# Layer 2 of image 0: the symmetric half for 10 of its 28 block pairs, in five transposed runs among the taps of layer 1, with column sums added by transfers

## The chip, the cores and the metric

The kernel runs on one core of a Trainium2 chip. The metric is the device time of one execution in microseconds (us), the median of several. The core has five engines with an instruction queue each: TensorE (PE, matrix products; its weight loads are shown as PEld), VectorE (DVE), ScalarE (ACT), GpSimd (POOL) and SyncE (SP, which here only issues transfers). Each engine works through its own queue in order and meets the others at semaphores. Data lie in SBUF (128 partitions); products go to PSUM.

## The reference, cut to what matters

Four images of 64 x 64 positions and 64 channels pass through four layers: an attention (layer 0), a convolution block (layer 1: norm, two pointwise products with a depthwise 3x3 convolution between them, a gate, and a second norm with two more pointwise products), a second attention without any weights (layer 2), and a last one (layer 3). The change is in layer 2:

```python
def _L2_conv_ref(x):
    B, C, H, W = x.shape
    N = H * W
    xf = x.reshape(B, C, N)
    scores = jnp.einsum('bci,bcj->bij', xf, xf)
    attn = jax.nn.softmax(scores, axis=-1)
    out = jnp.einsum('bcj,bij->bci', xf, attn).reshape(B, C, H, W)
    return out + x
```

The sum over c runs over the 64 rows, i and j over the 4096 pairs of the other two axes. The matrix of scores is the product of a matrix with itself, so it is symmetric, and so is its exponential before the division by the row sums: the block (g, h) is the transpose of the block (h, g).

## The kernel before, in words

The program is written out by hand as one list of items. A stage (layer 0, 2 or 3 of an image) appends items; `at(i, fn)` hangs work behind item i. Beside them run two lanes of generators, `conv` (layer 1 of an image) and `misc` (small things such as `features2`, which makes the copy `ko` that layer 2 takes its scores from). A lane has a clock: `tick(us)` moves it on by what an item is said to last, each `yield us` in the generator says how much clock its piece takes, and a piece is issued when the clock has come to it. So the numbers in `tick` and `yield` set the places at which layer 1's instructions stand between those of the stage, on every engine.

The order of stages is: layer 0 of the images 0 to 3; layer 2 of image 0; then layer 2 of image 1, layer 3 of image 0, layer 2 of image 2, and so on. Layer 1 of image b is run by the lane `conv` beside the stage after its layer 0. Layer 1 of image 3 therefore falls into layer 2 of image 0. In it `norm` (L1164 to L1191) sends eight broadcasts through SP, `pointwise` with pw1 is written to a padded tile by ACT (L1222), and the depthwise convolution is done by DVE: for each of two halves r and four column groups j nine taps, k = 0 to 8, over 128 x 1024 elements (the first at L1236, the others at L1238 and L1241), each adding to the one before. Then come the gate (L1249), a second `norm`, and pw3 and pw4 (L1205, L1284 to L1293).

Layer 2 divides the 4096 columns into eight blocks of 512. A block takes two steps. One step is a group of four 64x512 score products on PE into one 128x1024 PSUM slot, its exponential on ACT into a tile `e`, and a group of four 64x512 products of x with `e`. A group shows as eight records in the trace, PE's products being in two passes.

- Image 0 uses `layer2` (L1312 to L1372): all 8 x 8 blocks in 128 steps (32 items of four), 32 steps for each 1024 columns. The exponential is one ACT instruction of 128x1024 (L1336). The products (L1348) of 32 steps stay in a pair of PSUM accumulators; at their end ACT copies one, DVE adds the other (L1356), PE turns the result with four transposes (`turn`, L1361) and DVE copies it (L1364). `close2` (L1375 to L1385) divides by the row sums; it runs in four places of the next stage and has no PE work.
- The images 1 to 3 use `layer2s`: 72 steps. Of each pair of blocks only one is made; the products with the transposed block are made from `turned`, a copy of `e` with its 32x32 squares transposed by DVE (L1458, one instruction a step), by `turned_products` (L1509: 64 products, a "transposed run", for four steps). The two groups of accumulators are added by DVE into a tile A in SBUF (L1483). POOL adds the tiles `e` of a row block into `esum` (L1469, L1471), since the row sums of the transposed blocks are the column sums of these; `spread_sums` brings them to `cs` on DVE (L1477, L1478). `weights` (L1423) lays x out for the runs by 16 transfers of 32 KB on SP for each row block. A is cleared by POOL (L1539). `close2s` (L1556 to L1580) has four small products, 32 PE transposes, four multiplications and eight additions.

Tiles come from pools that are used in turn: `new_e` gives one of six buffers of 128x2048 (two steps to a buffer), `new_acc` the one pair of accumulators, `new_big` one of five large tiles, `new_ps` a PSUM slot. A buffer is written again only when everything that reads it is done.

Of the kernel before, what the change touches and what calls it, by code (L numbers as in the profile page):

```python
# [691 lines left out]
def fast_path(ctx: ExitStack, tc: tile.TileContext, a: dict, out: bass.AP, bad):  # L692
# [392 lines left out]
    def layer0(b):  # L1085
# [51 lines left out]
        def item(t):  # L1137
            tiles[t] = (
                [new_e() for _ in range(2)], sm.tile([128, C], F32, tag="vq", name="vq", bufs=4),
                sm.tile([128, 4], F32, tag="zs", name="zs", bufs=4),  # L1140
            )
            for g in range(4):
                if g == 2 and between:
                    between.pop()()
                score(t, g)
                late.append(lambda g=g: product(t, g))
                conv.tick(2.3)
                misc.tick(1.8)
                if g == 0 and t:
                    scale(t - 1)  # L1150
                follow()
            if t == 31:
                scale(t)
# [45 lines left out]
    def layer1(b):  # L1199
# [16 lines left out]
        for r in (1, 0):  # L1216
# [11 lines left out]
            for j in range(4):  # L1228
                w0 = 16 * j
                y1 = new_t("y1").rearrange("p (w h) -> p w h", h=H)  # L1230
                for k in range(9):
# [3 lines left out]
                    if k == 0:  # L1235
# [9 lines left out]
                    yield 1.8  # L1245
# [66 lines left out]
    def layer2(b):  # L1312
        x, m, first = X[:, b], im[b], len(items)
        xw = x.rearrange("p (w h) -> p w h", h=H)
        m.ph = None
        m.zs = sm.tile([128, 32, 4], F32, tag="zs2", name="zs2")
        es, acc = {}, {}
        quads = ((0, 0), (1, 0), (0, 1), (1, 1))

        def scores(n):  # L1320
            ib = n // 8
            if n == 0 and b:
                take_slots(0, 1, 2)
            for jb in range(4 * (n % 8), 4 * (n % 8) + 4):
                ps = new_ps()
                for r, c in quads:
                    rows_ = slice(64 * r, 64 * r + 64)
                    mm(  # L1328
                        ps[64 * c : 64 * c + 64, bass.ts(r, 512)],
                        m.ko[rows_, 128 * jb + 64 * c : 128 * jb + 64 * c + 64],  # L1330
                        m.ko[rows_, bass.ts(2 * ib + r, 512)], start=True, stop=True,
                    )
                if jb % 2 == 0:
                    e = new_e()
                es[n, jb] = e[:, bass.ts(jb % 2, 1024)]
                act(es[n, jb], ps, AF.Exp, bias=SHIFT2, accum_out=m.zs[:, jb, ib : ib + 1])  # L1336
                follow(0)
                conv.tick(2.5)
                misc.tick(1.8)

        def products(n):
            ib = n // 8
            if n % 8 == 0:
                acc[0], acc[1] = new_acc(), new_acc()
            for jb in range(4 * (n % 8), 4 * (n % 8) + 4):
                for r, c in quads:
                    rows_ = slice(64 * r, 64 * r + 64)
                    mm(  # L1348
                        acc[r][64 * c : 64 * c + 64, :], xw[rows_, jb, :],
                        es[n, jb][rows_, bass.ts(c, 512)], start=jb == 0, stop=jb == 31,  # L1350
                    )
            if n % 8 == 7:
                if m.ph is None:
                    m.ph = new_big("ph")
                nc.scalar.copy(m.ph[:, 2048:2560], acc[0])
                nc.vector.tensor_add(m.ph[:, 2048:2560], m.ph[:, 2048:2560], acc[1])  # L1356

        def turn(ib):
            ps = new_ps()
            for i in range(4):  # L1360
                nc.tensor.transpose(  # L1361
                    ps[:, bass.ts(i, 128)], m.ph[:, 2048 + 128 * i : 2176 + 128 * i], ident
                )
            nc.vector.tensor_copy(  # L1364
                m.ph[:, bass.ts(ib, 512)].rearrange("p (r q h) -> p q r h", r=2, q=4),
                ps[:, 0:512].rearrange("p (q r h) -> p q r h", q=4, r=2),
            )

        for n in range(32):
            items.append((lambda n=n: scores(n), 0.0))  # L1370
            at(first + n + (2 if n == 0 and b > 1 else 1), lambda n=n: products(n))
            if n % 8 == 7:  # L1372
                at(first + n + 2, lambda n=n: turn(n // 8))

    def close2(b):  # L1375
        x, m = X[:, b], im[b]
        nc.vector.tensor_reduce(sums2[:, b, :], m.zs, AX.X, ALU.add)
        rz = sm.tile([128, 32], F32, tag="rz2", name="rz2")
        nc.vector.reciprocal(rz, sums2[:, b, :])
        for i in range(4):  # L1380
            d = m.ph[:, bass.ts(i, 512)].rearrange("p (w h) -> p w h", h=H)
            nc.vector.tensor_mul(d, d, rz[:, bass.ts(i, 8)].unsqueeze(2).to_broadcast([128, 8, H]))
            xs = x[:, bass.ts(i, 512)]
            nc.vector.tensor_add(xs, xs, m.ph[:, bass.ts(i, 512)])
            yield 2.0 if i < 3 else 9.0  # L1385

    SIDES = [[(7, (h + 1) % 7), ((h + 2) % 7, (h + 3) % 7)] for h in range(7)] + [[]]  # L1390

    def layer2s(b, when_free):
# [5 lines left out]
        used = {}  # L1398
        steps = []
        for h in (7, 0, 1, 2, 3, 4, 5, 6):  # L1400
            own = [(h, h, u, None, None) for u in range(2)]
            other = [
                (h, g, u, pi, 2 * gi + u)
                for pi, pair in enumerate(SIDES[h]) for gi, g in enumerate(pair) for u in range(2)
            ]
            steps += other + own if h == 6 else own + other
        st = {"e": {}, "T": {}, "esum": {}}
        begin = [next(n for n in range(72) if steps[n][0] == h) for h in range(7)]
        begin[0] = 2
        run_of = {k: i for i, k in enumerate((h, pi) for h in range(8) for pi in range(len(SIDES[h])))}  # L1410

        def slot(g, t):
            k = used[g, t] = used.get((g, t), -1) + 1
            c = 16 * g + 4 * t if g < 7 else 112 + 8 * t
            return m.zs[:, c + k : c + k + 1]

        def weights(h):
            if h == 0:
                st["xr"] = xn.tile([128, 2048], F32, tag="xn", name="xn")
# [7 lines left out]

        def score(n):
            h, g, u, pi, ti = steps[n]
            if n == 0:  # L1430
                take_slots(0, 1, 2)
                m.zs = sm.tile([128, 144], F32, tag="zs2", name="zs2")
# [17 lines left out]
        def turned(n):  # L1450
            h, _, _, pi, ti = steps[n]
            if pi is None:
                return
            k = run_of[h, pi] % 2
# [7 lines left out]
        def column_sums(n):  # L1462
            h, _, _, pi, ti = steps[n]
            if pi is None or (pi, ti) == (0, 0):
                return
            if (pi, ti) == (0, 1):
                st["esum"][h] = new_e("esum")
            esum = st["esum"][h][:, 0:1024]
            nc.gpsimd.tensor_add(esum, st["e"][n - 1] if (pi, ti) == (0, 1) else esum, st["e"][n])  # L1469
            if (pi, ti) == (len(SIDES[h]) - 1, 3):  # L1470
                nc.gpsimd.tensor_add(esum[:, 0:512], esum[:, 0:512], esum[:, 512:1024])  # L1471

        def spread_sums(h):
            if h == 0:
                m.cs = sm.tile([128, 128], F32, tag="cs2", name="cs2", bufs=1)
            esum = st["esum"][h]
# [8 lines left out]
        def products(n):  # L1485
            h = steps[n][0]
            mine = [i for i in range(72) if steps[i][0] == h]
            if n == mine[0]:
                st["acc"] = new_acc(), new_acc()
            for r, c in quads:  # L1490
                rows_ = slice(64 * r, 64 * r + 64)
                jb = 4 * steps[n][1] + 2 * steps[n][2] + c
                mm(  # L1493
                    st["acc"][r][64 * c : 64 * c + 64, :], xw[rows_, jb, :],
                    st["e"][n][rows_, bass.ts(c, 512)], start=n == mine[0], stop=n == mine[-1],
                )
            if n == mine[-1]:
# [3 lines left out]
        def turned_products(h, pi):  # L1501
            T, slots = st["T"][run_of[h, pi] % 2], [new_ps(), new_ps()]
# [10 lines left out]
            view = m.A.rearrange("p (g t q j) -> p q g t j", g=8, t=4, q=4)  # L1513
            for i in range(2):
                for gi, g in enumerate(SIDES[h][pi]):
                    add_to(
                        view[:, 2 * i : 2 * i + 2, g],
                        slots[i].rearrange("p (q g t j) -> p q g t j", q=2, g=4, t=4)[:, :, gi],
                    )

        last_of = {}
        for n, (h, _, _, pi, ti) in enumerate(steps):
            if ti == 3:
                last_of[n] = (h, pi)
        todo = []

        def item(n):
            h = steps[n][0]
            if n == 6:
                weights(0)  # L1530
            if n + 1 in begin[2:] or n == 8:
                weights(1 if n == 8 else begin.index(n + 1))
# [7 lines left out]
            if n >= 4:  # L1540
# [3 lines left out]
            if n - 2 in last_of:  # L1544
                turned_products(*last_of[n - 2])
                if run_of[last_of[n - 2]] == 12:
                    when_free()
# [531 lines left out]
```

## Time and profile before

The median of three runs is 2469.21 us (2469.07 to 2469.25). The profiled execution took 2469.9 us.

| what | us |
|---|---|
| profiled execution: its own time | 2469.9 |
| span in the profile, first to last instruction | 2467.7 |
| PE busy in the span | 2431.4 |
| ACT busy | 1645.1 |
| DVE busy | 1429.1 |
| POOL busy | 511.4 |
| window 1013 to 1285 (layer 2 of image 0): PE busy | 269.7 of 272 |
| the same: DVE / ACT / POOL busy | 123.4 / 170.9 / 3.5 |

The span is one execution on the chip. A row of a group view gives the line of the kernel, the engine, the operation with its tiles (output <- input, by the program's names), the count, then busy us and the mean ns of one, then how long the engine stood idle just before instructions of the group, and for whom. In a timeline a row has the start in us, the duration in us, and in square brackets the idle time before it with the instruction that ended it. A window row has the stretch, its length, and for PE, PEld, DVE, ACT and POOL the busy us and the count, then the granted clock of PE, the busy share of the DMA engines and GB/s. PE's instructions overlap, so durations of neighbours add up to more than the time that they take; the distance from start to start is what one costs.

### The profile page before, as it was taken

The numbers are of one execution on the slowest core, as the hardware profiler recorded it, in microseconds if no ns is written. First come the engines' busy times: TensorE is split into PE (matmuls) and PEld (weight loads), VectorE is DVE, ScalarE is ACT, GpSimd is POOL, SyncE is SP. The second block draws the span as 40 slices with busy tenths as digits, with TensorE's granted clock in tenths as the row PEclk, the third lists the DMA queues.
The fourth block names the chain that finished last, engine by engine and source line by source line (L and its number), as shares of the span: only waits on it lengthen the run. The fifth ranks groups of instructions, "written<-read, shape, count | busy, mean of one in ns | idle before, by whom it ended". The sixth has DMA issues, their size and how long they took to land.

```text
span 2467.7 us, 62283 instructions
## 1 busy us (share of the span) xinstructions
PE 2431.4 (99%) x27037; PEld 919.6 (37%) x27037; DVE 1429.1 (58%) x1723; ACT 1645.1 (67%) x2982; POOL 511.4 (21%) x349
## 2 busy tenths in 40 slices
PE   9999999999999999999999999999999999999998
PEld 3343463336433643334334442134431244421113
DVE  2010277228822773177217657877668876678886
ACT  4666766676666676666654459954479754579996
POOL 2000000000000000000007662246631365622110
PEclk9999999999999999999999999999999999999999
DMA  3000000010000000000000017610065400296554
GB/s 79 1 18 1 18 1 18 18 19 1 18 18 18 1 19 18 9 11 18 18 18 19 19 45 155 138 27 20 19 138 121 87 19 19 64 173 142 117 120 118
DMA packets 59982, 117.43 MB, mean 48 GB/s; under 512 B 11468, under 2 KB 30645, under 8 KB 59701
## 3 DMA queue, kind: packets, MB, share of 16 engines
q0 software_dynamic: 19712, 69.77, 14.2%
q1 hardware_dynamic: 39237, 41.75, 7.5%
q8 instruction: 214, 3.51, 0.6%
q10 hardware_dynamic: 752, 1.85, 0.2%
q14 instruction: 67, 0.55, 0.1%
HBM read 4.80 MB, written 4.19 MB: 4 GB/s over the span
## 4 chain that ended last, share of the span: by engine, by line
PE 89%; DVE 5%; ACT 4%; issue 1%; SPq 0%; DVEq 0%; ACTq 0%; DMA 0%
PE PS L1121 18%; PE PS L1095 17%; PE PS L1657 9%; PE PS L1718 8%; PE PS L1440 7%; PE PS L1493 7%; PE PS L1509 6%; PE PS L1348 4%; PE PS L1328 4%; DVE tg L1709 3%; PE PS L1205 2%; ACT e L1668 1%; ACT e L1100 1%; PE PS L1170 1%; PE PS L1063 1%
## 5 line engine op out<-in xcount | busy, mean ns | idle before, releaser
L1100 ACT ACTIVATE e<-PS 128x1024 f32<-128x1024 f32 x512 | 524.2, 1024 | 331.5 <-PE PS L1095 300.0
L1121 PE MATMUL PS<-e,vq 64*64 64x512 f32 x4096 | 573.8, 592 | 0.0
L1095 PE MATMUL PS<-X,q 64*64 64x512 f32 x4096 | 571.6, 591 | 1.8 <-DVE X L979 1.7
L1668 ACT ACTIVATE e<-PS 128x512 f32<-128x512 f32 (+2 forms) x588 | 500.9, 921 | 60.5 <-PE PS L1657 39.7
L1445 ACT ACTIVATE e<-PS 128x512 f32<-128x512 f32 x432 | 254.0, 594 | 287.2 <-PE PS L1440 270.2
L1709 DVE TENSOR_TENSOR tg<-tg,e 128x2048 f32<-128x2048 f32 x172 | 393.9, 2290 | 42.7 <-ACT e L1668 31.2
L1238 DVE SCALAR_TENSOR_TENSOR y<-pad,vec,y 128x1024 f32<-128x1024 f32 x240 | 308.1, 1284 | 8.8 <-ACT pad L1222 1.4
L1469 POOL TENSOR_TENSOR esum<-esum,e 128x1024 f32<-128x1024 f32 x126 | 299.1, 2373 | 53.5 <-ACT e L1445 46.7
L1657 PE MATMUL PS<-tg,ph 32*64 32x512 f32 x4096 | 295.3, 613 | 2.8 <-DVE A L1483 2.7
L1095 PEld LDWEIGHTS PS<-X,q 64*64 64x64 f32 x4096 | 184.5, 133 | 257.2 <-issue 178.2
L1121 PEld LDWEIGHTS PS<-e,vq 64*64 64x64 f32 x4096 | 184.4, 133 | 250.4 <-issue 152.6
L1718 PE MATMUL PS<-e,tg 128*32 128x512 f32 x2048 | 272.5, 604 | 0.0
L1458 DVE STREAM_TRANSPOSE turned<-e 128x1024 f32<-128x1024 f32 x168 | 206.6, 1238 | 86.3 <-ACT e L1445 86.3
L1440 PE MATMUL PS<-ko 64*64 64x512 f32 x1728 | 236.1, 598 | 0.0
L1493 PE MATMUL PS<-e,X 64*64 64x512 f32 x1728 | 232.1, 590 | 1.5 <-DVE A L1483 1.3
L1539 POOL MEMSET A<- 128x4096 f32 x3 | 11.2, 3737 | 1013.1 <-PE PS L1121 1013.1
L1108 DVE TENSOR_REDUCE sums<-zs 128x1 f32<-128x4 f32 x128 | 19.7, 154 | 301.7 <-ACT e L1100 301.3
L1336 ACT ACTIVATE e<-PS 128x1024 f32<-128x1024 f32 x128 | 129.8, 1023 | 85.3 <-PE PS L1328 82.1
L1690 POOL DMA_DIRECT2D xn<-e x116 | 101.3, 898 | 290.4 <-ACT e L1668 196.8
L1509 PE MATMUL PS<-turned,xn 32*64 32x256 f32 x5376 | 157.2, 377 | 2.5 <-DVE sums L1564 1.6
L1483 DVE TENSOR_TENSOR A<-PS,A 128x256 f32<-128x256 f32 (+1 forms) x216 | 92.3, 477 | 96.7 <-PE PS L1509 76.1
L1657 PEld LDWEIGHTS PS<-tg,ph 32*64 32x64 f32 x4096 | 64.0, 129 | 222.4 <-ACT e L1668 183.8
(224 smaller groups left out, 1937.3 us busy)
## 6 DMA issues: line engine op xcount, KB each, us to landing
xn<-e POOLq DMA_DIRECT2D x132, 512.0 KB, 5.4
xn<-X SPq DMA_DIRECT2D x336, 32.0 KB
xn<-t SPq DMA_DIRECT2D x64, 128.0 KB
ph<-tg SPq DMA_DIRECT2D x64, 128.0 KB
ko<-ko SPq DMA_DIRECT2D x32, 128.0 KB
xr<-in_x_dram SPq DMA_DIRECT2D x13, 256.0 KB
q<-q SPq DMA_DIRECT2D x12, 256.0 KB
out_dram<-o SPq DMA_DIRECT2D x7, 256.0 KB
```

What stands on the lines that cost most here:

```text
L1095: mm(ps[64 * c : 64 * c + 64, bass.ts(r, 512)], m.q[rows_, 128 * t + 64 * c : 128 * t + 64 * c + 64], x[rows_, bass.ts(g, 512)], start=Tru ...
L1100: act(es[g // 2][:, bass.ts(g % 2, 1024)], ps, AF.Exp, bias=SHIFT0, accum_out=zs[:, g : g + 1],)
L1121: ins = mm(PS[64 * s : 64 * s + 64, 2048 + 512 * j : 2560 + 512 * j], vq[rows_, :], es[j // 2][rows_, k : k + 512], start=t == 0 and i < 2 ...
L1238: stt(y1, win, wt, y1, ALU.mult, ALU.add)
L1440: mm(ps[64 * c : 64 * c + 64, bass.ts(r, 512)], m.ko[rows_, k : k + 64], m.ko[rows_, bass.ts(h, 512)], start=True, stop=True,)
L1469: nc.gpsimd.tensor_add(esum, st["e"][n - 1] if (pi, ti) == (0, 1) else esum, st["e"][n])
L1493: mm(st["acc"][r][64 * c : 64 * c + 64, :], xw[rows_, jb, :], st["e"][n][rows_, bass.ts(c, 512)], start=n == mine[0], stop=n == mine[-1],)
L1509: mm(slots[q // 2][64 * c : 64 * c + 64, o : o + 256], st["xr"][rows_, w : w + 64], T[rows_, bass.ts(e, 256)], start=e < 2, stop=e >= 14,)
L1657: mm(PS[64 * c : 64 * c + 64, bass.ts(banks[k], 512)], m.ph[32 * k : 32 * k + 32, 128 * mc + 64 * c : 128 * mc + 64 * c + 64], m.th[32 * k ...
L1668: act(e[:, 512 * lo : 512 * k], PS[:, 512 * banks[lo] : 512 * banks[lo] + 512 * (k - lo)], AF.Exp,)
L1709: nc.vector.tensor_add(esum, esum, e)
L1718: mm(st["y"][32 * k : 32 * k + 32, :], m.gx[:, i % 32, :], es[i][:, bass.ts(k, 512)], start=mc == 0, stop=i % 32 == 31,)
```

## The change

`layer2` and `layer2s` become one function `layer2(b, when_free)`, and `close2` and `close2s` one function `close2`. The images 1 to 3 follow the list FULL, which is the order they had. Image 0 follows a new list PART: row blocks in the order 0, 1, 2, 3, 4, 7, 6, 5, of which three have transposed runs: block 0 the pairs of blocks (1, 2) and (3, 4), block 6 (1, 2), block 5 (1, 2) and (3, 4). Ten block pairs are thus made once, the other 18 twice: 54 blocks or 108 steps in place of 128. The row blocks have 16, 10, 10, 12, 12, 16, 16 and 16 steps; the runs' own steps are 4 to 7, 12 to 15, 82 to 85, 94 to 97 and 102 to 105, and the products of a run stand two steps behind its last step.

For image 0 this means further: the exponential is done in two halves of 128x512; the results are gathered in A by DVE instead of being turned by PE; the tiles `xr` (the weights) and `esum` are taken from the pool of `e`; there is one `turned` tile instead of two; and the column sums are made by transfers that POOL issues (20 of 512 KB), the first of a row block a copy, the others adding in place, each waiting for the one before on the same tile. POOL then adds the two halves of `esum`, and `spread_sums` follows five steps after a row block's last transposed step (in items 20 and 90, and in item 3 of the next stage). `weights` runs at steps 0, 60 and 64 of image 0 (48 transfers). `close2` of image 0 runs, as for the others, at the items 8, 12, 22, 32 and 42 of layer 2 of image 1.

The lane numbers change with it: `conv` moves on by 2.5 for 2.3 in each step of layer 0, and by 2.9 for 2.5 in each step of layer 2 of image 0; a tap takes 2.05 for 1.8 of the clock. The first tap (k = 0) of image 3 goes from DVE to ACT. `features2` of image 1 starts at step 50 of 108 (before: item 16 of 32).

```diff
-                conv.tick(2.3)
+                conv.tick(2.5)
...
-                    if k == 0:
+                    if k == 0 and b == B - 1:
+                        act(y1, win, AF.Identity, bias=V("L1_conv_dw_b", r), scale=wt)
+                    elif k == 0:
                         nc.vector.tensor_scalar(y1, win, wt, V("L1_conv_dw_b", r), ALU.mult, ALU.add)
...
-                    yield 1.8
+                    yield 2.05
...
-    def layer2(b):
...
-    def layer2s(b, when_free):
+    SIDES = [[(7, (h + 1) % 7), ((h + 2) % 7, (h + 3) % 7)] for h in range(7)]
+    FULL = [(7, [7])] + [(h, [h] + SIDES[h]) for h in range(6)] + [(6, SIDES[6] + [6])]
+    PART = [
+        (0, [0, 5, (1, 2), 6, 7, (3, 4)]), (1, [1, 2, 3, 4, 7]), (2, [2, 1, 3, 4, 7]), (3, [3, 1, 2, 4, 6, 7]),
+        (4, [4, 1, 2, 3, 6, 7]), (7, [7, 0, 1, 2, 3, 4, 5, 6]), (6, [6, 0, 3, (1, 2), 4, 5, 7]),
+        (5, [5, (1, 2), 0, 6, (3, 4), 7]),
+    ]
+
+    def layer2(b, when_free=None):
...
+        spread_at = {mine_t[h][-1] + 5: h for h in m.mirrored}
+        late_start, tiles = (6, 1) if b == 0 else (4, 2)
...
-                st["xr"] = xn.tile([128, 2048], F32, tag="xn", name="xn")
+                st["xr"] = new_e("xr") if b == 0 else xn.tile([128, 2048], F32, tag="xn", name="xn")
...
+        if b == 0:
+            weights_at = {0: 0, 60: 6, 64: 5}
+        else:
+            weights_at = {6: 0, 8: 1, **{mine[h][0] - 1: h for h in range(2, 7)}}
...
+            if b == 0:
+                nc.gpsimd.dma_start(out=esum, in_=e, **({} if k == 0 else {"accum_op": ALU.add}))
+            else:
+                nc.gpsimd.tensor_add(esum, st["e"][mine_t[h][0]] if k == 1 else esum, e)
...
+            if b == 0:
+                follow(0)
+                conv.tick(2.9)
+                misc.tick(1.8)
+            if n >= late_start:
...
+        at(len(items), lambda: [products(todo.pop(0)) for _ in range(2)])
+        for n, h in spread_at.items():
+            if n >= len(steps):
+                at(len(items) + (1 if b else 3), lambda h=h: spread_sums(h))
...
-            misc_from[f + 16] = [features2(b + 1)]
+            misc_from[f + 50] = [features2(b + 1)]
...
+            turns = close2(b - 1)
+            for i in (8, 12, 22, 32, 42):
+                at(f + i, lambda turns=turns: next(turns))
```

## The prediction

> **What bounds the kernel now.** I read the profile from the outside in: engines, then the stage that is edited, then PE's own waits in it, then single instructions. The page's first and fourth parts first.
>
> ```profile
> PE 2431.4 (99%) x27037; PEld 919.6 (37%) x27037; DVE 1429.1 (58%) x1723; ACT 1645.1 (67%) x2982; POOL 511.4 (21%) x349
> PE 89%; DVE 5%; ACT 4%; issue 1%; SPq 0%; DVEq 0%; ACTq 0%; DMA 0%
> ```
>
> PE is the bound. Any time saved must be PE work taken away, and any us for which PE is made to wait is lost. The busy time by window for the edited stage (layer 2 of image 0; PE, PEld, DVE, ACT, POOL) and PE's list of waits in it and in the stage behind it:
>
> ```profile
> 1013.00:1285.00 272.00, 269.74 (x2390) 95.81 (x2382) 123.43 (x134) 170.93 (x313) 3.51 (x1) 1.00 0.08 17
> PE PS L1361 <- ACT ko L1308: 1.7, 1, 1.7
> PE PS L1493 <- DVE A L1483: 1.3, 1, 1.3
> PE PS L1361 <- DVE ph L1356: 0.6, 1, 0.6
> ```
>
> The stage has no slack on PE; DVE and ACT have it on average, and POOL is empty. So the average asks for less PE work, and the question is the moments at which PE needs DVE. One such moment is in the trace of before, where layer 2 of image 1 changes its row block (timeline of DVE, then of PE):
>
> ```profile
> 1291.13 1.25 DVE L1458 STREAM_TRANSPOSE turned<-e 128x1024 f32<-128x1024 f32 x1 [4.01 <-ACT e L1445]
> 1292.30 1.45 DVE L1483 TENSOR_TENSOR A<-PS,A 128x512 f32<-128x512 f32 x2
> 1290.66 1.04 PE L1440 MATMUL PS<-ko 64*64 64x512 f32 x8
> 1293.01 2.31 PE L1493 MATMUL PS<-e,X 64*64 64x512 f32 x13 [1.31 <-DVE A L1483]
> ```
>
> There is one pair of accumulators. PE has one group of scores (0.86 us) to do between the last product of a row block and the first of the next. DVE, in order, did one transpose of 1.25 us before the two adds, and PE stood for 1.31 us.
>
> **PE work.** Two groups and a turned run, from PE's timeline in the same stage:
>
> ```profile
> 1302.54 3.71 PE L1509 MATMUL PS<-turned,xn 32*64 32x256 f32 x128
> 1306.18 1.09 PE L1440 MATMUL PS<-ko 64*64 64x512 f32 x8
> 1307.09 1.04 PE L1493 MATMUL PS<-e,X 64*64 64x512 f32 x8
> 1307.95 1.04 PE L1440 MATMUL PS<-ko 64*64 64x512 f32 x8
> ```
>
> From start to start a group takes 0.86 us, a step (score and product) 1.714, a run 3.64, 3.8 with both seams. The changed stage has 108 steps for 128: 20 x 1.714 = -34.3. Five runs at 3.72: +18.6. The 16 transposes of turn go (a set of four takes 0.66 us at 1285.73): -2.6. close2 of image 0 gets what the later images have, 32 transposes and 4 column matmuls (280 and 218 ns busy in L1572 and L1561, two overlapping): 4.4 + 0.3 = +4.7. Sum -13.6 us. With the sets of waits above, which belong to turn and to the old row-block change, gone (1.7 + 0.6 + 1.3): -17.2.
>
> **ACT.** Its exponentials become two halves, 594 ns each for 1.023 us whole: 1.16 us a step against PE's 1.714. Eight first taps of image 3 come to ACT (the nearest row is L1284, 1.11 us), 9 us spread over the stage. No bound; but ACT is in order, so each such tap ends some 1.9 us behind the score at which it is issued: the half of an exponential in hand, the next one, its own 1.1.
>
> **DVE at the changes of row block.** Now the accumulators are added to A in SBUF (L1483: two of 685 ns), between the taps of image 3:
>
> ```profile
> L1238 DVE SCALAR_TENSOR_TENSOR y<-pad,vec,y 128x1024 f32<-128x1024 f32 x60 | 77.0, 1284 | 3.4 <-ACT pad L1222 1.4
> 1119.55 10.60 DVE L1238 SCALAR_TENSOR_TENSOR y<-pad,vec,y 128x1024 f32<-128x1024 f32 x8
> ```
>
> A tap takes 1.32 us of DVE and is issued every 2.05/2.9 steps, 1.21 us of PE. DVE cannot run ahead, since ACT opens each group of nine, and falls back 0.1 us a tap. Count from the first score of the stage, in PE work. First change inside taps (steps 25 to 26): ACT's tap is issued at 54.3 (22 scores, 20 products, two runs, 10.8 of image 3's norm and pointwise groups) and ends at 56.2; seven taps of 1.32 and two halves (1.41) end at 66.9, the adds at 68.3. PE ends its last product at 65.4 and the next score at 66.2: 2.1 us of waiting. In the same way 35 to 36: ACT at 78.9 (the earlier wait included), five taps from 80.8, adds done 88.8, PE there at 85.8: 3.0. 47 to 48: 115.0 against 112.8: 2.2. 59 to 60, behind copies of features2: 1.5 to 3.3, 2.4. Sum 9.7. The two changes behind the taps (blocks 7 to 6, 6 to 5) have only the adds: 2 x 0.69 + 0.1 - 0.86 = 0.6, and 1.3 with a transpose ahead as above; 1.0 each, 2.0. The change 15 to 16 is covered by a run of 3.6 us: 0.4. Start of the stage 0.5, features2's copies between taps 0.7 (both estimates: half a tap each, 0 to 1.3). close2 of image 0 puts four multiplications and eight adds on DVE ahead of transposes of image 1: 1.0, between 0 and 2.
>
> **POOL and the transfers.** Column sums were on POOL (L1469, 2373 ns); here 20 transfers of 512 KB, each waiting for the one before on the same tile. From the page's DMA part and groups:
>
> ```profile
> xn<-e POOLq DMA_DIRECT2D x132, 512.0 KB, 5.4
> L1690 POOL DMA_DIRECT2D xn<-e x116 | 101.3, 898 | 290.4 <-ACT e L1668 196.8
> L1539 POOL MEMSET A<- 128x4096 f32 x3 | 11.2, 3737 | 1013.1 <-PE PS L1121 1013.1
> ```
>
> With no other beside it one landed 4.6 us after issue (1565.71 to 1570.31), and POOL goes on 0.3 later: 4.9 a link. The first eight (steps 4 to 15) end near 54 us of the stage, when DVE reaches spread_sums: free. The last chain issues its second four from step 102: counted from step 94, 45 us, then POOL's add 1.3 and, behind it on POOL, the memset of A of image 1, 3.7. Image 1's first adds to A want it about 3.4 us earlier: +3.4. [...]
>
> The 48 weight transfers more on SP: 0.63 us each by L1423, 32 of them (20 us) ahead of eight broadcasts of image 3's norm, of which taps come only at 42 us: free. If that cover failed, the taps and not PE would be late. Layer 0's lane at 2.5 and 2.05 shifts taps there by a step or two where DVE is half idle (131 of 255 us): 0, between -2 and +2. The e pool loses two of six buffers to xr and esum; a pair lives 8 steps, 13.7 us, and transfers of the pairs of steps 6 and 7 land at 28 us, before step 14 needs them at 37: 0.
>
> **Sum.** Waits 9.7 + 2.0 + 0.4 + 0.5 + 0.7 + 1.0 + 3.4 = 17.7. The profiled run took 2469.9 us (span 2467.7 and 2.2 around it); 2469.9 - 17.2 + 17.7 = 2470.4; the median shown is 0.7 lower, so 2469.7.
>
> **Rivals.** First, covered: DVE overtakes while PE stands, ACT's taps come earlier than I put them, the memset is in time. For it: 123 of 272 us on DVE. Against it: the order of engines, and 1.31 us for a single transpose. With 6 us of waits for 17.7: 2458. Second, the other side: the transfers' links. If one takes over some 5.4 us (the page's median, where two run at once), the eight end at 58 and every further us of chain stands in front of spread_sums on DVE, with taps and the adds of 25 to 26 behind it; at 6.3 a link (5.4 and a second issue of 0.9) the chain is 11 us late and the last one as well: two waits of 5 to 9 us, 2480 to 2488. It decides from 5.2 up. Third: the taps' lateness grows from group to group as on a saturated DVE: the four waits double, 2479.
>
> **How the numbers follow.** Walk 0.45, covered 0.25, links 0.18, saturated 0.12. About 0.2% (4.9 us) is what can be told from no change. Walk's own range is 2463 to 2477 (waits 11 to 25): of its 0.45, 0.11 faster, 0.23 same, 0.11 slower. Covered: 0.21 faster, 0.04 same. Links: 0.17 and 0.01 same. Saturated: 0.10 slower, 0.02 same. Together 0.32, 0.30, 0.38. The range leaves out the tails of covered and of links: 2456 to 2483.
>
> **What would show it.** In the profile after: 864 records for 1024 in the scores of image 0's stage, five runs near 3.7 us, PE waits on the adds to A of 2 to 3 us four times among the taps and 3 us at image 1's first change; POOL's waits on transfers of 4 to 5 us. Wrong if PE's waits in the stage add up to under 8 us (then 2460), if PE waits on exponentials that wait for transfers, or if a link takes over 5.4.

## The result, and the profile after

The changed kernel takes 2482.8 us (median of six runs, 2481.6 to 2484.3) for 2469.2: ratio 1.0054, 95% interval 1.0041 to 1.0067, slower by 13.6 us, or 0.54%. It is on the side of the prediction's second rival and inside its range by 0.2 us; two of the six executions lie beyond its end. The profiled execution took 2481.6 us, 11.7 more than that of before. The page of the changed kernel:

```profile
PE 2428.8 (98%) x27381; PEld 932.6 (38%) x27381; DVE 1466.9 (59%) x1778; ACT 1651.6 (67%) x3162; POOL 534.1 (22%) x374
PE 87%; DVE 6%; ACT 4%; issue 1%; SPq 1%; DMA 0%; POOL 0%; DVEq 0%; ACTq 0%
```

And the window of image 0's layer 2 that was shown of before:

```profile
1013.00:1285.00 272.00, 256.61 (x2686) 108.28 (x2682) 154.68 (x176) 177.05 (x491) 21.84 (x23) 0.98 0.28 58
```

Two things stand there. PE is busy 256.6 us of the window where it was busy 269.7, so it now stands idle more; and the granted clock of the window, the third number from the end, is 0.98 where it was 1.00. PE's waits from 1010 to 1320 us:

```profile
PE PS L1439 <- DVE A L1431: 15.7, 5, 5.1
PE PS L1380 <- DVE A L1431: 1.5, 1, 1.5
PE PS L1292 <- DVE u L1288: 1.0, 1, 1.0
PE PS L1380 <- ACT e L1385: 0.6, 1, 0.6
PE PS L1439 <- DVE X L1133: 0.6, 1, 0.6
```

That is 19.4 us in sum; the prediction walked to 17.7. So the sum of the waits is nearly the one that was foretold, though not each of its terms, and yet the time is 13 us off. The longest wait shows two reasons. DVE's timeline, then PE's, at the change from row block 1 to block 2:

```profile
1080.78 0.71 DVE L1425 STREAM_TRANSPOSE esum<-esum 128x512 f32<-128x512 f32 x1 [3.14 <-POOL esum L1417]
1081.59 0.69 DVE L1426 TENSOR_REDUCE cs<-esum 128x16 f32<-128x512 f32 x1
1082.20 9.20 DVE L1240 SCALAR_TENSOR_TENSOR y<-pad,vec,y 128x1024 f32<-128x1024 f32 x7
1091.43 1.42 DVE L1243 SCALAR_TENSOR_TENSOR yg<-pad,vec,y 128x512 f32<-128x512 f32 x2
1092.76 1.48 DVE L1431 TENSOR_TENSOR A<-PS,A 128x512 f32<-128x512 f32 x2
```

```profile
1086.40 1.23 PE L1439 MATMUL PS<-e,X 64*64 64x512 f32 x8
1087.25 1.23 PE L1380 MATMUL PS<-ko 64*64 64x512 f32 x8
1093.59 2.68 PE L1439 MATMUL PS<-e,X 64*64 64x512 f32 x8 [5.11 <-DVE A L1431]
1095.33 2.65 PE L1380 MATMUL PS<-ko 64*64 64x512 f32 x8
1097.03 1.81 PE L1439 MATMUL PS<-e,X 64*64 64x512 f32 x8
1098.30 1.39 PE L1380 MATMUL PS<-ko 64*64 64x512 f32 x8
```

First, DVE stood 3.1 us for the column sums at `spread_sums` (L1425), with seven taps and then the adds behind it; so PE waited 5.1 us, not 2.1. Second, when PE goes on, a group takes 1.74, 1.70 and 1.27 us from start to start for 0.86. The windows around it (granted clock is the third number from the end) say why:

```profile
1087.00:1090.00 3.00, 1.48 (x15) 0.43 (x7) 2.93 (x3) 3.00 (x8) 0.00 (x0) 1.00 0.00 0
1090.00:1093.00 3.00, 0.00 (x0) 0.00 (x0) 2.93 (x5) 0.36 (x2) 0.00 (x0) 0.67 0.00 0
1093.00:1096.00 3.00, 2.41 (x9) 1.03 (x13) 2.86 (x4) 0.00 (x0) 0.00 (x0) 0.50 0.02 5
1096.00:1099.00 3.00, 3.00 (x24) 1.32 (x20) 2.93 (x3) 0.98 (x3) 0.00 (x0) 0.69 0.00 0
```

The clock was at one half for 2 x 3 x (0.33 + 0.50 + 0.31) = 6.8 us, of which 4.3 lay behind the restart: 2.1 us lost on top of the wait. The same happens behind the wait of 2.05 us at 1167 (half speed for 3.4 us: 1.7 lost) and behind the one of 4.15 us at 1292 (6.8 us, PE back at 1296.4: 3.1 lost). It does not happen behind the wait of 2.98 us at 1113. The sum is 6.9 us, which no row of before contained.

What sets the wait of 2.05 us, with a drop, apart from that of 2.98 us, with none, can be looked for in the same trace. The three stretches at half speed begin at 1091.02, 1169.53 and 1295.82 us and last 6.83, 3.41 and 6.83 us. Their starts lie 23 and 37 times 3.413 us apart; the estimate from these times is that the clock changes on a fixed grid of windows of that length. Cut along this grid, the windows around 1113, then those around 1167:

```profile
1111.50:1114.92 3.42, 1.93 (x19) 0.53 (x11) 3.31 (x4) 2.53 (x8) 0.00 (x0) 1.00 0.00 0
1114.92:1118.33 3.41, 1.92 (x14) 1.02 (x18) 3.27 (x5) 0.00 (x0) 0.00 (x0) 1.00 0.00 0
1166.12:1169.53 3.41, 1.36 (x13) 0.34 (x6) 3.27 (x4) 2.01 (x8) 0.00 (x0) 1.00 0.00 0
1169.53:1172.95 3.42, 3.42 (x17) 1.26 (x19) 3.35 (x4) 0.00 (x0) 0.00 (x0) 0.50 0.00 0
```

The longer wait is shared by two windows, in each of which PE still worked 1.9 us. The shorter one falls into a single window with 1.36 us of work, and the next window runs at half speed.

The wait at image 1's first row-block change, DVE's timeline and then POOL's:

```profile
1292.15 0.71 DVE L1425 STREAM_TRANSPOSE esum<-esum 128x512 f32<-128x512 f32 x1 [4.39 <-POOL esum L1417]
1295.61 1.49 DVE L1431 TENSOR_TENSOR A<-PS,A 128x512 f32<-128x512 f32 x2 [0.87 <-POOL A L1478]
```

```profile
1290.86 1.26 POOL L1417 TENSOR_TENSOR esum<-esum 128x512 f32<-128x512 f32 x1 [4.29 <-DMA xn<-X]
1292.07 3.50 POOL L1478 MEMSET A<- 128x4096 f32 x1
```

As the prediction had it: POOL's add stands behind the last transfer, the memset of A behind the add, and the adds to A behind the memset. But DVE itself stood for the same chain until 1292.15, at `spread_sums` in front of the adds; the memset alone accounts for the last 0.87 us.

### The profile page after: what moved, and what is told of

Read it like the earlier page. It is cut to its first block, busy times and chain, and to the rows that moved or that the text cites. A ratio compares the mean times of both kernels' runs of the same rounds, so it can differ in the third digit from the quotient of the medians.

```text
span 2479.7 us, 63372 instructions
## 1 busy us (share of the span) xinstructions
PE 2428.8 (98%) x27381; PEld 932.6 (38%) x27381; DVE 1466.9 (59%) x1778; ACT 1651.6 (67%) x3162; POOL 534.1 (22%) x374
## 4 chain that ended last, share of the span: by engine, by line
PE 87%; DVE 6%; ACT 4%; issue 1%; SPq 1%; DMA 0%; POOL 0%; DVEq 0%; ACTq 0%
PE PS L1121 17%; PE PS L1095 17%; PE PS L1380 10%; PE PS L1439 10%; PE PS L1612 9%; PE PS L1673 8%; PE PS L1456 7%; DVE tg L1664 2%; PE PS L1205 2%; ACT e L1623 1%; DVE y L1240 1%; ACT e L1385 1%; SPq L1357 1%; ACT e L1100 1%; PE PS L1170 1%
## 5 line engine op out<-in xcount | busy, mean ns | idle before, releaser
L1100 ACT ACTIVATE e<-PS 128x1024 f32<-128x1024 f32 x512 | 524.2, 1024 | 333.1 <-PE PS L1095 300.1
L1385 ACT ACTIVATE e<-PS 128x512 f32<-128x512 f32 x648 | 380.7, 595 | 380.2 <-PE PS L1380 361.7
L1439 PE MATMUL PS<-e,X 64*64 64x512 f32 x2592 | 373.6, 597 | 16.5 <-DVE A L1431 15.7
L1380 PE MATMUL PS<-ko 64*64 64x512 f32 x2592 | 376.1, 600 | 2.2 <-DVE A L1431 1.5
L1240 DVE SCALAR_TENSOR_TENSOR y<-pad,vec,y 128x1024 f32<-128x1024 f32 x240 | 308.0, 1283 | 29.8 <-ACT y L1236 22.4
L1398 DVE STREAM_TRANSPOSE turned<-e 128x1024 f32<-128x1024 f32 x188 | 231.4, 1239 | 112.5 <-ACT e L1385 112.5
L1439 PEld LDWEIGHTS PS<-e,X 64*64 64x64 f32 x2592 | 111.9, 134 | 198.9 <-issue 166.4
L1108 DVE TENSOR_REDUCE sums<-zs 128x1 f32<-128x4 f32 x128 | 19.7, 154 | 270.0 <-ACT e L1100 269.7
L1431 DVE TENSOR_TENSOR A<-PS,A 128x256 f32<-128x256 f32 (+1 forms) x252 | 110.5, 486 | 112.2 <-PE PS L1456 91.2
L1380 PEld LDWEIGHTS PS<-ko 64*64 64x64 f32 x2592 | 105.5, 133 | 167.4 <-issue 142.2
```

The source lines that it names most:

```text
L1100: act(es[g // 2][:, bass.ts(g % 2, 1024)], ps, AF.Exp, bias=SHIFT0, accum_out=zs[:, g : g + 1],)
L1240: stt(y1, win, wt, y1, ALU.mult, ALU.add)
L1380: mm(ps[64 * c : 64 * c + 64, bass.ts(r, 512)], m.ko[rows_, k : k + 64], m.ko[rows_, bass.ts(h, 512)], start=True, stop=True,)
L1385: act(e[:, bass.ts(r, 512)], ps[:, bass.ts(r, 512)], AF.Exp, bias=SHIFT2, accum_out=slot(g, 2 * u + r),)
L1439: mm(st["acc"][r][64 * c : 64 * c + 64, :], xw[rows_, 4 * g + 2 * u + c, :], st["e"][n][rows_, bass.ts(c, 512)], start=n == mine[h][0], st ...
```

## The experiments

The first four take one suspect each out of the changed kernel. The waits are named by the step at which PE stands for the adds of a finished row block: 28, 38, 50 and 62 for the row blocks 1 to 4 of image 0. Behind each median stand, in brackets, the lowest and the highest run, then the ratio to the kernel before and its 95% interval.

**PE kept busy where it waits.** Extra score groups that nothing reads are issued into an idle slot at the five changes.

```diff
+            spare = new_ps() if again else None
+            for _ in range(again):
+                for r, c in quads:
...
+                    mm(
+                        spare[64 * c : 64 * c + 64, bass.ts(r, 512)], m.ko[rows_, 0:64],
+                        m.ko[rows_, bass.ts(h, 512)], start=True, stop=True,
+                    )
```

> The changed kernel with extra score groups that PE issues into an idle PSUM slot just where it would stand and wait for the adds to A: 5, 3, 1 and 2 groups at steps 28, 38, 50 and 62 of image 0 and 4 at step 5 of image 1 (15 x 0.86 = 12.9 us of PE work that nothing reads). Theory of the clock (PE's granted clock falls to one half for some us behind three of the waits, worth 2.1 + 1.5 + 3.2 = 6.8 us): the waits are filled, the clock stays at 1.0, 2474 to 2478 us. Rival (the time is lost in the waits alone, the clock is a side effect): no gain, 2482 to 2485 us.

Measured 2480.0 us (2476.2 to 2483.5; 1.0037, 1.0023 to 1.0051). In the profiled run, 2483.5 us, the waits for A in the stage were filled (none over 0.9 us) and the clock stayed at 1.00 around them. PE's timeline at the first of them, and PE's longest waits in the whole run:

```profile
1087.90 4.66 PE L1394 MATMUL PS<-ko 64*64 64x512 f32 x40
1092.62 1.45 PE L1448 MATMUL PS<-e,X 64*64 64x512 f32 x5
1093.53 0.59 PE L1381 MATMUL PS<-ko 64*64 64x512 f32 x1
```

```profile
PE PS L1292 <- DVE u L1288: 3.3, 1, 3.3
PE PS L1621 <- ACT e L1632: 3.2, 1, 3.2
```

The first of these waits was 1.0 us in the changed kernel; the second, in layer 3, was 0.7. Each now had a stretch at half speed behind it, of 3.4 and 6.8 us. The median lies between the two expectations, and so this run alone doesn't decide. Its executions, though, order themselves by the mean granted clock: 2476.2 us at 0.998, 2478.6 to 2481.1 at 0.997, 2483.5 at 0.996. A thousandth of the mean clock is 5 us at half speed, 2.5 us lost.

**Column sums by POOL.** The transfers go; nothing else.

```diff
-            if k == (0 if b == 0 else 1):
+            if k == 1:
...
-            if b == 0:
-                nc.gpsimd.dma_start(out=esum, in_=e, **({} if k == 0 else {"accum_op": ALU.add}))
-            else:
-                nc.gpsimd.tensor_add(esum, st["e"][mine_t[h][0]] if k == 1 else esum, e)
+            nc.gpsimd.tensor_add(esum, st["e"][mine_t[h][0]] if k == 1 else esum, e)
```

> The changed kernel with image 0's column sums by POOL additions (2.37 us each, 17 of them) in place of the 20 transfers; nothing else. Theory of the chain (DVE stood 3.1 us for the sums at the first spread, and the memset of A of image 1 came late behind the last chain): the 5.1 us wait at step 28 falls to about 2, the 4.2 us wait at image 1's first change to under 1, and the clock drops behind both go: 2469 to 2473 us. Rival (DVE's taps alone make both waits): the waits stay, 2481 to 2484 us. Second rival (POOL's additions slow DVE's taps): taps over 1.35 us, 2484 us or more.

Measured 2473.6 us (2471.5 to 2475.8; 1.0016, 1.0007 to 1.0026): 9.3 less than the changed kernel. The first two lines of PE's waits in the same stretch:

```profile
PE PS L1436 <- DVE A L1428: 9.5, 5, 3.0
PE PS L1436 <- ACT e L1385: 1.9, 1, 1.9
```

The 5.1 us wait became 1.9 (for an exponential), the one at image 1's change 1.5, and 3.0, 1.5 and 2.1 stayed: the theory of the chain, though 0.6 us over the range that it expected. Taps took 1317 ns in the mean for 1283, and a new wait of 1.5 us stands at the end of row block 0.

**The first tap back on DVE.**

```diff
-                    if k == 0 and b == B - 1:
-                        act(y1, win, AF.Identity, bias=V("L1_conv_dw_b", r), scale=wt)
-                    elif k == 0:
+                    if k == 0:
```

> The changed kernel with the first tap of image 3 back on DVE (8 x 0.81 us more DVE work, ACT's part gone). Theory that DVE is late because each group of taps waits for ACT (1.9 us behind the score): the waits at steps 38, 50 and 62 shrink by about 1 us each, 2478 to 2481 us. Theory that DVE simply has too much to do in the tap phase: they grow by 0.8 us or more each, 2484 to 2488 us.

Measured 2475.7 us (2473.9 to 2478.7; 1.0028, 1.0017 to 1.0040): 7.2 less, better than the first theory's range and against the second. The waits at steps 38 and 50 are gone and the one at 62 is 0.7 us; the wait behind the late chain stays, 5.6 us. DVE works 6.4 us more and is less late, as it no longer stands for ACT: 22.4 us of waiting for the first tap in the changed kernel.

**The accumulators out by ACT.** ACT copies them and POOL adds the copies to A, so that PE needs nothing of DVE at these changes.

```diff
-            if n == mine[h][-1]:
+            if n == mine[h][-1] and b == 0 and h not in (0,):
+                o, cols = new_e("o"), m.A[:, bass.ts(h, 512)]
+                for r in range(2):
+                    nc.scalar.copy(o[:, bass.ts(r, 512)], st["acc"][r])
+                for r in range(2):
+                    nc.gpsimd.tensor_add(cols, cols, o[:, bass.ts(r, 512)])
+            elif n == mine[h][-1]:
```

> The changed kernel with the accumulators of image 0's row blocks 1 to 7 copied out by ACT (two of 0.59 us) into a buffer of the e pool, and added to A by POOL; DVE's adds behind the taps go there. Theory that the waits come from DVE's order: those at steps 28, 38, 50 and 62 fall to about 0.7 us each, with the clock drops behind them: -4.4 -2.1 -2.3 -0.8 -1.4 -1.5 = -12.5, 2469 to 2472 us. Rival (the e pool is too small for one more buffer, or ACT is as late as DVE): waits of 2 us and more for exponentials, 2480 us or more. The 4.2 us wait at image 1's first change stays in both.

Measured 2473.7 us (2471.9 to 2478.4; 1.0016, 1.0006 to 1.0025): 9.2 less. At step 28 PE waited 1.2 us, at 38, 50 and 62 under what the list shows. Others came in their place: 3.6 us for u (L1288, in the second part of layer 1), which stands on DVE behind a spread that waits for the second chain of transfers; 1.8 us for a copy of features2 on ACT, which itself stood 3.6 us for a copy on DVE behind taps; 1.8 us for an exponential; and 5.6 at image 1's change. The time lies in neither range: the waits at the four steps fell as the first theory had it, and what it gained went in part to the others.

**The price of a wait, by itself.** In the kernel before, two or four DVE transposes are put ahead of the adds at image 1's first change, where PE waits 1.3 us anyway; the output doesn't use them.

```diff
             if n == mine[-1]:
+                if b == 1 and h == 7:
+                    spare = new_e("spare")
+                    for _ in range(2):
+                        nc.vector.transpose(spare[:, 0:1024], st["e"][n])
                 for r in range(2):
```

> The kernel before with two DVE transposes more (1.25 us each, into a buffer that nothing reads) ahead of the adds of image 1's first row block, where PE waits 1.3 us already. PE's wait becomes 3.8 us. Theory that a wait costs its own length: +2.5, 2471.5 to 2472.5 us. Theory that PE's granted clock falls behind a long wait: between +2.5 and +4.2 with runs that differ by about 1.7 us, as the wait fills a clock window or not, 2472.5 to 2474 us.

> The same with four transposes: PE's wait becomes 6.3 us. A wait costs its own length: +5.0, 2474 to 2475 us. The clock falls to one half for two windows of 3.4 us, the second of which holds PE work: +6.7 to +8.4, 2476 to 2478 us.

Measured 2473.6 us (2473.0 to 2474.3; 1.0017, 1.0007 to 1.0026) and 2476.4 (2475.2 to 2476.9; 1.0028, 1.0017 to 1.0039) against 2469.5: +4.1 for 2.4 us more waiting and +7.0 for 5.0. With two, the trace has one stretch of 3.4 us at half speed, all of it behind the restart: 1.7 us lost. PE's timeline with four, and windows at the restart:

```profile
1290.51 1.04 PE L1440 MATMUL PS<-ko 64*64 64x512 f32 x8
1297.82 4.48 PE L1493 MATMUL PS<-e,X 64*64 64x512 f32 x16 [6.27 <-DVE A L1483]
1301.29 2.03 PE L1440 MATMUL PS<-ko 64*64 64x512 f32 x8
```

```profile
1294.00:1297.00 3.00, 0.00 (x0) 0.00 (x0) 2.93 (x3) 0.00 (x0) 1.30 (x1) 0.78 0.00 0
1297.00:1300.00 3.00, 2.18 (x9) 0.92 (x13) 2.60 (x4) 0.00 (x0) 0.00 (x0) 0.50 0.00 0
1300.00:1303.00 3.00, 3.00 (x20) 1.02 (x16) 0.00 (x0) 0.00 (x0) 0.00 (x0) 0.59 0.00 0
```

Sixteen records, two groups, took 3.47 us for 1.72; of 6.8 us at half speed 4.6 lay behind the restart, 2.3 lost. In these two kernels, whose runs lie within 2 us of each other, the surcharge on the wait is 1.7 and 2.0 us. In PE's list of waits of this stretch nothing changed but the length of the one. "A wait costs its length" is refuted, and the clock's part is shown apart from the chain and the taps.

**The two helpful edits together,** column sums by POOL and the first tap on DVE:

> The changed kernel with both edits that helped: image 0's column sums by POOL additions and the first tap of image 3 on DVE. If the chain of transfers and ACT's place were separate causes, the waits at steps 38, 50 and 62 (3.0 + 1.2 + 2.1 us with the sums by POOL alone) go down to about 1 us in sum and one or two clock drops with them: 2466 to 2469 us. If POOL's additions beside the taps (1.32 us a tap for 1.28) eat it: 2470 to 2473 us.

Measured 2467.0 us (2466.2 to 2467.6; 0.9990, 0.9981 to 1.0000), the first expectation. The causes add: 15.8 us less than the changed kernel, for 9.3 and 7.2 alone. PE still waited 8.0 us for A, the longest 2.3.

**The chain left in, its reader moved.** First tap on DVE; block 0 keeps its transfers, but its spread is issued at step 29, and blocks 6 and 5 are summed by POOL:

```diff
-        spread_at = {mine_t[h][-1] + 5: h for h in m.mirrored}
+        spread_at = {mine_t[h][-1] + (14 if b == 0 == h else 5): h for h in m.mirrored}
...
-            if b == 0:
+            if b == 0 == h:
```

> The changed kernel with the first tap on DVE, row block 0's sums by transfers as it has them but its spread at step 29 for 20 (behind the adds of step 28), and the sums of blocks 6 and 5, behind the taps, by POOL. Theory that the late chain holds up DVE only because the spread stands in front of taps and adds: the 5.6 us wait at step 28 falls to 1 us or less, and the 3.1 us at image 1's first change goes: 2464 to 2468 us. If the chain holds something else (the exponentials that reuse its buffers): 2470 us or more.

Measured 2468.3 us (2465.9 to 2468.5; 0.9993, 0.9984 to 1.0003), a little over the range. The wait at step 28 fell from 5.6 to 3.2 us, not to 1, and one of 2.5 came at 38, behind the moved spread. DVE did not stand for the chain any more: the spread follows a tap at 1096.80 without idle time. What is left is DVE's own queue of taps, copies and adds. PE's waits at the ends of the row blocks 0 to 4 sum to 6.6 us here and to 6.4 in the kernel with both helpful edits. So a late chain does its harm through what stands behind its reader on DVE, and moving the reader takes that part away and no more.

**The lane numbers of layer 0.** On the pair of helpful edits, 2.3 and 1.8 again; image 3's taps keep 2.05.

```diff
-                conv.tick(2.5)
+                conv.tick(2.3)
...
-                    yield 2.05
+                    yield 2.05 if b == B - 1 else 1.8
```

> Column sums by POOL, first tap on DVE, and the lane numbers of layer 0 as before (2.3 a step, 1.8 a tap; only image 3's taps keep 2.05). It prices the term that the prediction put at nothing, between -2 and +2: if the later start of image 0's layer 2 (1019.7 for 1017.3 us) is only work that moved ahead of it, 2466 to 2468 us as without this edit; if it is a loss, 2464 to 2465 us.

Measured 2470.4 us (2470.0 to 2472.2; 1.0003, 0.9994 to 1.0012), 3.4 more than without this edit and outside both expectations: the new numbers are a gain. With the old ones PE's products of image 3's norm (L1170) come right behind the product that finishes the X they read, which DVE still has to write (L1133). That is a wait that the lists of the others don't have, and half speed for 3.4 us follows it:

```profile
PE PS L1170 <- DVE X L1133: 4.5, 1, 4.5
```

**Towards a faster kernel.** ACT's copies on top of the two helpful edits, then also at block 0 of image 0 and block 7 of the images 1 to 3 (the condition becomes `b == 0 or h == 7`):

> Column sums by POOL, first tap on DVE, and the accumulators of row blocks 1 to 7 copied out by ACT and added to A by POOL. DVE's order no longer reaches PE: the waits at steps 28, 38 and 62 (2.3 + 1.2 + 0.8 us with the first two edits alone) fall to about 0.7 each, 2464 to 2466 us. Rival: ACT, with 1.2 us more at each change, holds PE as DVE did (the copies of features2 or the exponentials wait 2 us), 2467 to 2470 us.

> As the last version (column sums by POOL, first tap on DVE, accumulators out by ACT), now also at row block 0 of image 0 and at block 7 of the images 1 to 3, where PE still waited 2.3 and 1.5 us for DVE with a clock drop behind each. Theory that every such wait costs its length and, where it fills a clock window, up to 1.7 us more: -1.6 -0.8 and up to -3.4 for the clock, 2459 to 2462 us. Rival: the e pool, which then lends buffers to xr, esum and the copies at once, holds the exponentials: 2464 us or more.

Measured 2464.0 us (2462.6 to 2464.9; 0.9977, 0.9967 to 0.9987), as expected, and 2456.2 (2455.7 to 2459.6; 0.9950, 0.9936 to 0.9964), below the range: 13.1 us faster than the kernel before and 26.7 faster than the change as it was made. PE's waits and the stage's window in the last:

```profile
PE PS L1378 <- DVE A L1426: 4.8, 2, 3.3
PE PS L1378 <- ACT e L1383: 0.6, 1, 0.6
PE PS L1434 <- DVE X L1133: 0.6, 1, 0.6
PE PS L1434 <- ACT o L1441: 0.3, 1, 0.3
```

```profile
1013.00:1285.00 272.00, 265.31 (x2817) 105.52 (x2809) 172.58 (x176) 187.81 (x534) 85.52 (x43) 1.00 0.10 23
```

No more than 0.3 us of waiting is left at the changes of row block (the 4.8 us are for the slots of transposed runs), and the clock stays at 1.00, though one of these waits is 3.3 us long. DVE and ACT are busier in this window than in the kernels of the diff and are no bound.

## Why the prediction was right in its shape and 13 us short

That the time lies in the range is luck in good part. The sum said 2469.7, no change, and the upper end at 2483 was there for the rival of the slow links, which came true only by half. By the profiled runs the sum is 11.2 us short (2470.4 for 2481.6): 1.7 for the waits, 6.9 for the clock, which is in no term, and the rest for PE's work, point by point:

*PE's work, -13.6, and the waits of before, -3.6:* the spans of the two profiles differ by +12.0. PE's whole lists of waits add up to 24.0 us before and 38.1 after, which is +14.1, and the clock took 6.9. So -9.0 remains for PE's work and its seams, and the work was taken 4.6 us too high. The waits of before did go, 4.0 us of them, and 1.3 us of waits elsewhere with them. Of the 4.6 us, 1.3 are restarts: from the last score before a wait to the first product behind it 6.34 us pass where group and wait explain 5.97, and 0.5, 0.2 and 0.2 more than explained at 1112, 1166 and 1291. The rest was not traced to a cause. The same reckoning (span, less all waits, less the time lost to half speed, an estimate from each trace) gives -13.3 for the last kernel, in which ACT releases PE at every change of row block of image 0 and at the first of the images 1 to 3, and between -8 and -11 for the other kernels with the change and no extra PE work. So the work that was counted is there; that the changes of row block hold the rest is likely and not shown.

*DVE at the changes:* the waits at steps 38, 50 and 62 were put at 3.0, 2.2 and 2.4 and came to 2.98, 1.45 and 2.05. The mechanism, ACT's place and the order of DVE, is shown by the first tap on DVE and by the copies on ACT. The changes 7 to 6 and 6 to 5 (2.0), the copies of features2 (0.7) and close2 (1.0) cost nothing that the list shows. That these terms came to nothing hides the excess at step 28 in the sum of the waits. The start cost 1.2 for 0.5, and 1.0 for u (L1288) and 1.5 for PSUM slots at the stage's end were not foreseen.

*The transfers:* "the first eight end near 54 us of the stage, when DVE reaches spread_sums: free" is the first step that failed. From one issue to the next a link was put at 4.9 us; through the first chain it took 5.8 in the mean (eight links from 1032.86 to POOL's add at 1079.47). The longest, 8.6 us, runs from 1036.76 to 1045.34, while SP issues the eight broadcasts of the norm (1036.47 to 1045.20) and the DMA engines are busy to 0.85. That this traffic is the cause is read from the times and was not tested alone. The chain ended 59.8 us into the stage, for 54. That cost 3 us of wait at step 28, as the run with the sums by POOL shows. It is the rival "links", which was to decide from 5.2 us a link and was worked out at 6.3, at about half its size; the prediction's own sign of being wrong, a link over 5.4, came true. In the last chain the second four links took 5.8 us each as well, and its 3.4 came to 4.15.

*The clock* is the larger failure, and it is in no step: the sum took every wait at its own length, because before has no wait of PE over 1.7 us behind its setup and a granted clock of 1.00 in every window shown. Behind three of the five waits of 1.5 to 5 us for A, half speed cost 6.9 us more in the profile. The run with idle PE time filled could not settle this; the two kernels with one lengthened wait do: their traces show 1.7 and 2.3 us lost to half speed, for surcharges of 1.7 and 2.0. The runs agree on the length of the stretches at half speed: 6.83, 3.41 and 6.83 us in the changed kernel, 3.4 with two transposes ahead of the adds and 6.8 with four. The length of a wait alone does not tell whether one follows: 2.05 us of waiting at 1167 had a drop and 2.98 at 1113 none. Likewise, of two waits of 2.3 us in the kernel with both helpful edits the one at 1072 had a drop and the one at 1094 none. Even 1.54 us, at image 1's change, had a drop in the kernel with the reader moved and none in the one with both helpful edits. That a wait's place in the grid decides is an estimate from the one trace cut along it; no run tests it alone.

*Layer 0's lane*, put at 0 and between -2 and +2, was worth -3.4 us on the one base where it was measured, by where it puts image 3's norm.

## What to carry to other kernels

When PE is the bound, price a wait of 1.5 us or more at its length and, where the clock drops behind it, at what half speed costs too (here 1.7 us behind waits of 2.05 and 3.71 us, 2.1 to 3.1 behind waits of 4.15 to 6.27, nothing behind one of 2.98), and look for an engine that can release PE out of turn: in the last kernel two copies on ACT did with at most 0.3 us of waiting what two adds on DVE, behind taps, did with 1.5 to 5. In a chain of transfers on one tile, each waiting for the last, take the links beside other traffic as longer than alone (here 5.8 us in the mean and 8.6 at worst, beside eight broadcasts, for the 5.0 and 5.1 of the links from 1247.22 and 1252.25, beside which SP issued nothing), and look at what stands behind the reader of the chain on its engine. A first link moved to a less busy engine can cost more than it frees, if everything behind it has to wait for that engine's turn.

## What the runs showed of the hardware that was not expected

DVE's taps and POOL's adds took longer beside each other. With the copies on ACT and POOL's adds to A, seven taps that ran beside two of these adds took 11.0 us in place of 9.2; DVE's timeline, then POOL's, of that kernel:

```profile
1093.97 9.20 DVE L1240 SCALAR_TENSOR_TENSOR y<-pad,vec,y 128x1024 f32<-128x1024 f32 x7
1104.53 11.00 DVE L1240 SCALAR_TENSOR_TENSOR y<-pad,vec,y 128x1024 f32<-128x1024 f32 x7
```

```profile
1107.44 4.36 POOL L1448 TENSOR_TENSOR A<-A,o 128x512 f32<-128x512 f32 x2 [13.95 <-ACT o L1446]
```

POOL's two adds took 4.36 us, for the 2.60 of the two at 1285.81, behind the taps. The mean of 60 taps is 1375 ns for 1283 in the changed kernel, whose POOL only issues transfers in that stretch. With the column sums by POOL it is 1317 ns: 60 x 34 ns, 2.0 us, is what the transfers spare DVE, and less than their lateness cost (9.3 us by the run with the sums by POOL, clock included). POOL's issues of transfers did not take longer beside taps: 0.86 us each at 1067.10 and 1073.46 in the changed kernel, with taps running, as at 1051.36, with DVE idle, for 898 ns in the mean in layer 3.
